# GINE layer 0: rows beside four pairs of blocks, edges beside the pair ahead, sums carried pair by pair

## The chip, the cores and the metric

The kernel runs on one core of a Trainium2 chip. The metric is the device time of one launch in microseconds (us); the figure for the kernel before is the median of three runs. The engines are named as in the profile: PE (TensorE: matmuls and transposes), DVE (VectorE), ACT (ScalarE), POOL (GpSimd, which also issues the gathers), SP (SyncE, which issues the other transfers). Each engine takes its instructions in the order in which the program has them, and waits at one whose inputs are not there.

## The reference, cut to what matters

The program has four stages on x of 10000 nodes by 512 features in float32: a relational graph network, a mixture of experts, a GINE network of four layers, and a quantized feed-forward layer. Each adds its result to x and takes the layer norm of x as its input. The change lies in the third:

```python
def _gine_layer(x, src, dst, edge_attr, eps, We, be, W1, b1, gamma, beta, W2, b2):
    e = edge_attr @ We + be
    m = jax.nn.relu(x[src] + e)
    agg = jax.ops.segment_sum(m, dst, num_segments=x.shape[0])
    h = ((1.0 + eps) * x + agg) @ W1 + b1
    mu = jnp.mean(h, axis=0)
    var = jnp.mean(jnp.square(h - mu), axis=0)
    h = (h - mu) * jax.lax.rsqrt(var + BN_EPS) * gamma + beta
    h = jax.nn.relu(h)
    return jax.nn.relu(h @ W2 + b2)
```

There are 5000 edges, sorted by target (dst). The first layer's x is the layer norm of what the mixture of experts left. The mean and variance run over all nodes, so the second product (W2) starts only when the first (W1) is done for every node.

## The kernel before, in words

**Layout.** The features lie transposed in SBUF in one tile, `big` (named feat in the profile): 128 partitions, four feature chunks, 10000 node columns. Nodes are permuted so that those with edges come first: 40 edge tiles of 128 slots feed exactly the first 5120 columns, tile t the 128 columns from 128 t. The columns are worked in ten *pairs* (of blocks of 512): pairs 0 to 8 have 1024 columns, pair 9 has 784. Pairs 0 to 4 are the ones that edges feed; the order of work is 5, 6, 7, 8, 9, 0, 1, 2, 3, 4. A copy of the rows, node by node, is kept in DRAM as `xg_d`, for the edges to gather x[src] from.

**Layer 0's rows** (loop over `order`, L1472 its transposes). A block of four tiles of 128 nodes is gathered into `x_in` (POOL, `gather`, L612), normalized (`layernorm`: statistics L168 and L169 and the scaling L183 on DVE, the square root L171 on ACT), stored to `xg_d` (SP, L137) and transposed on PE through PSUM into `big` (L1472; evictions alternate between ACT L156 and DVE L158). `x_in` has two buffers. A buffer is free again when its block is stored and transposed.

**Edges** (`gine_edge_tile`). For each tile: gather 128 rows of `xg_d` (L612), add attr x We (DVE, L1232), in layer 0 also `be` (POOL, L1234; later layers have it in the rows), relu (ACT, L1235). A 128 x 128 matrix `same`, which marks edges of one target, sums them: in layer 0 it is made from a transpose of the keys on PE (L1241) and a comparison (DVE, L1242) and stored; later layers load it. Four matmuls (L1246) give the sums in PSUM; DVE adds them into `big` with (1 + eps) x (L1250; the last column apart, L1254), and ACT keeps the last column as the tile's tail (L1258). PSUM tiles of edges, row transposes and key transposes share the name ps_x and two buffers. An edge tile's gather needs all of `xg_d`; its result is needed by the product of the pair that it feeds.

**Carry** (`gine_carry`). Sums of one target may run over tiles. A scan on DVE over all 40 tails (L1267 to L1277) carries them on and adds them to the first column of the next tile.

**Products** (`product`). Each pair's 512 x 512 product is done with seven half-size products (a scheme of Strassen's kind), 56 PE instructions of 512 columns, all on L1311; ps_b, ps_d and ps_e are its PSUM tiles. It begins with two subtractions on DVE (L1334, L1335), has two operations on POOL (L1346, L1359), evictions on ACT (L1319) and sums on DVE (L1324 or L1326); for the first product, batch-norm statistics follow (L1394). It is a Python generator of seven steps.

**What sets the order.** `products` walks the generators of an order of pairs, starts each before the last step of the one ahead, and advances `beside` between steps. In layer 0 the program text has all rows first, then pairs 5 to 9 with the 40 edge tiles beside them, the carry, and pairs 0 to 4 with nothing beside; layers 1 to 3 have the same without the rows (theirs are written by the second product of the layer ahead, `gine_second`, `row_tile` L1419 to L1422). A scheduler then orders the instructions of each engine by its own reckoning: in layer 0 it put the products of pairs 5 to 9 among the rows, all but the end of pair 9. The engines' queues that matter here: POOL has gathers, the addition of `be` and two operations of every product; SP has the stores to `xg_d`, those of `same`, and loads of weights.

Of the kernel before, what the change touches and what calls it, by code (L numbers as in the profile page):

```python
# [30 lines left out]
PAIRS = [(p * 1024, 512) for p in range(N // 1024)] + [(N // 1024 * 1024, N % 1024 // 2)]  # L31
EB = EDGE_SLOTS // 512
# [30 lines left out]
def block_cols(b):  # L63
    return min(512, N - b * 512)
# [3 lines left out]
def gnn_ffn_kernel(ctx: ExitStack, tc: tile.TileContext, I, out, dram):  # L68
# [1158 lines left out]
    def gine_edge_tile(l, t, wk, px, we, be, scaled, tails):  # L1227
# [30 lines left out]
        nc.scalar.copy(tails[:, :, t], ps_a[:, :, P - 1])  # L1258

    def gine_carry(wk, tails):  # L1260

        co, _, passes, enters = (
            by_dst["carried"][:, i, None, :].to_broadcast([P, KC, ET]) for i in range(4)
        )
        through = wk.tile([P, KC, ET], F32, name="through", bufs=1)
        sums = wk.tile([P, KC, ET], F32, name="sums", bufs=1)
        nc.vector.tensor_copy(through, passes)  # L1267
        nc.vector.tensor_tensor(tails, tails, co, OP.mult)
        nc.vector.tensor_tensor_scan(
            sums.rearrange("p k t -> p (k t)"), through.rearrange("p k t -> p (k t)"),  # L1270
            tails.rearrange("p k t -> p (k t)"), 0.0, OP.mult, OP.add,
        )
        nc.vector.tensor_tensor(
            tails[:, :, 1:], sums[:, :, : ET - 1], enters[:, :, 1:], OP.mult
        )
        firsts = big[:, :, P : EDGE_SLOTS : P]
        nc.vector.tensor_add(firsts, firsts, tails[:, :, 1:])  # L1277
# [91 lines left out]
    def products(order, make, beside):  # L1369


        gens = [make(p) for p in order]
        next(gens[0])
        next(beside, None)
        for i, g in enumerate(gens):
            for _ in range(5):
                next(g)
                next(beside, None)
            if i + 1 < len(gens):
                next(gens[i + 1])  # L1380
                next(beside, None)
            next(g, None)
            next(beside, None)
        for _ in beside:
            pass
# [21 lines left out]
    def norm_pair(p, sm):  # L1407
        s0, w = PAIRS[p]
        for j in (1, 0):
            for fo in range(KC):  # L1410
                norm_relu(s0 + j * w, s0 + (j + 1) * w, sm, fo)
                yield
# [11 lines left out]
    def gine_second(l, A, banks, tmp, px, rows, be, sm, order):  # L1424

        def beside():


            for i in range(len(order) + 1):
                normed = norm_pair(order[i + 1], sm) if i + 1 < len(order) else iter(())  # L1430
                tiles = iter(())
                if i:
                    s0, w = PAIRS[order[i - 1]]
                    tiles = iter(range(s0 // P, (s0 + 2 * w + P - 1) // P))
                for step in range(7):
                    for _ in range(2 if step < 2 else 1):
                        next(normed, None)
                    for t in tiles:
                        row_tile(t, px, rows, be)
                        break  # L1440
                    yield
                for t in tiles:
                    row_tile(t, px, rows, be)

        for _ in norm_pair(order[0], sm):
            pass
        products(
            order, lambda p: product(p, A, banks, tmp, 1.0, b2c[:, l], True, lambda half, j: None), beside()
        )

    stats = wl.tile([P, KC, NB, 6], F32, name="stats")
    sm = wl.tile([P, KC, 4], F32, name="bn_sm")
    order = list(range(EB, NB)) + list(range(EB))
    pairs = list(range(EB // 2, len(PAIRS))) + list(range(EB // 2))
    with ExitStack() as s:
# [339 lines left out]
```

## Time and profile before

| | us |
|---|---|
| median of three runs (4684.91 to 4697.69) | 4692.14 |
| the profiled execution's own time | 4696.59 |
| its span, from first to last instruction | 4694.8 |
| PE busy | 4073.4 (87%) |
| DVE busy | 2848.6 (61%) |
| ACT busy | 1625.7 (35%) |
| POOL busy | 1569.1 (33%) |
| mean granted PE clock | 0.921 of full |

How to read it. Busy time is summed per engine over the span. PE's tenths are shares of a slice (one fortieth of the span), the granted clock likewise. A matmul row counts PE instructions; a product of float32 operands takes two. In a list of waits the three numbers are the total wait in us, how often, and the longest. In a timeline a line has start, length, engine, source line, operation, what it wrote and read, how many were merged, and in brackets the idle time ahead of it with what ended that. In a list of groups a line has the count, then busy us and mean ns, then idle time ahead of the group by what ended it.

### The profile page before, as it was taken

What the parts mean: (1) busy time and instruction counts of PE and PEld (TensorE: products, weight loads), DVE (VectorE), ACT (ScalarE), POOL (GpSimd) and SP (SyncE); (2) the same over time, 40 slices, a digit from 0 to 9 for tenths busy, and PEclk for the clock granted to TensorE, in tenths of its full rate; (3) what the DMA queues carried; (4) which work ended last, traced back from release to release, by engine and by line L of the source; (5) the groups of instructions that cost most, each with busy time, mean ns of one, the idle gap of its engine ahead of it and who ended that gap; (6) DMA issues with size and microseconds to landing.
All of it is one profiled execution on the core that took longest, in us unless ns stands there. A gap on an engine that the chain in (4) does not pass through costs nothing.

```text
span 4694.8 us, 42564 instructions
## 1 busy us (share of the span) xinstructions
PE 4073.4 (87%) x13624; PEld 2069.6 (44%) x13624; DVE 2848.6 (61%) x5806; ACT 1625.7 (35%) x2895; POOL 1569.1 (33%) x1127
## 2 busy tenths in 40 slices
PE   6899478897999936967769999999999999999997
PEld 3434234443444413434454455545455454544443
DVE  7887855554544574647754457645576455755776
ACT  4344112233333310112222623345233542334775
POOL 3434334441000046864552113311143111422443
PEclk9899789898999867988859999999999999999998
DMA  8777654457555315985420113201241022311332
GB/s 281 242 263 235 226 114 87 85 105 198 179 171 178 136 47 103 160 174 184 151 83 16 54 75 123 57 16 68 77 122 42 18 79 85 112 30 45 109 109 97
DMA packets 292814, 556.19 MB, mean 118 GB/s; under 512 B 40912, under 2 KB 71665, under 8 KB 291567
## 3 DMA queue, kind: packets, MB, share of 16 engines
q1 hardware_dynamic: 219328, 364.67, 23.0%
q0 software_dynamic: 73264, 188.79, 17.5%
q8 instruction: 111, 1.82, 0.2%
q14 instruction: 111, 0.91, 0.1%
HBM read 292.40 MB, written 260.95 MB: 118 GB/s over the span
## 4 chain that ended last, share of the span: by engine, by line
PE 36%; DVE 9%; DMA 4%; issue 3%; ACT 3%; POOL 2%; DVEq 0%; POOLq 0%; ACTq 0%
PE ps_b L1311 14%; PE ps_d L1311 8%; PE ps_o L1567 5%; PE ps_e L1311 4%; DMA x<-xg_d,gpos 3%; PE ps_x L1419 2%; PE ps_x L1246 2%; DVE stats L1394 1%; ACT feat L1405 1%; DMA x_in<-x_d,node_at 1%; DVE x L1232 1%; DVE feat L1250 1%; PE ps_q L1635 1%; DVE feat L1326 1%; POOL x_in L612 1%
## 5 line engine op out<-in xcount | busy, mean ns | idle before, releaser
L1311 PE MATMUL ps_b<-feat,w 128*128 128x512 f32 (+1 forms) x1120 | 499.3, 587 | 25.5 <-ACT feat L1405 25.5
L1311 PE MATMUL ps_d<-feat,w_s 128*128 128x512 f32 (+1 forms) x1120 | 503.1, 590 | 14.4 <-DVE feat L1335 14.4
L1319 ACT ACTIVATE feat<-ps_b,cols 128x512 f32<-128x512 f32 (+1 forms) x300 | 204.4, 683 | 591.2 <-PE ps_b L1311 586.7
L1346 POOL TENSOR_TENSOR feat<-feat 128x1024 f32<-128x1024 f32 (+1 forms) x70 | 163.4, 2335 | 710.4 <-DVE feat L1345 701.8
L1359 POOL TENSOR_TENSOR feat<-feat,p 128x1024 f32<-128x1024 f32 (+1 forms) x70 | 178.1, 2544 | 474.3 <-ACT feat L1319 474.3
L635 DVE SCALAR_TENSOR_TENSOR w<-basis,att,w 128x2048 f32<-128x2048 f32 x116 | 315.0, 2724 | 14.7 <-DMA basis<-in_L_gnn_basis 14.7
L740 PE MATMUL ps_o<-root,xT 128*128 128x512 f32 (+1 forms) x632 | 321.1, 620 | 0.0
L1311 PEld LDWEIGHTS ps_b<-feat,w 128*128 128x128 f32 x1120 | 206.5, 192 | 241.3 <-issue 201.1
L1311 PEld LDWEIGHTS ps_d<-feat,w_s 128*128 128x128 f32 x1120 | 208.0, 194 | 227.9 <-issue 193.6
L701 PE MATMUL ps_o<-w,aT 128*128 x656 | 304.8, 609 | 0.0
L1421 DVE TENSOR_TENSOR x_rows<-ps_x,be 128x512 f32<-128x512 f32 (+1 forms) x237 | 160.7, 685 | 218.4 <-PE ps_x L1419 218.2
L916 PE MATMUL ps_n<-root,rT 128*128 128x512 f32 (+1 forms) x632 | 289.6, 614 | 0.0
L1311 PE MATMUL ps_e<-feat,w 128*128 128x512 f32 (+1 forms) x560 | 264.9, 613 | 12.5 <-DVE feat L1277 12.5
L612 POOL DMA_INDIRECT x<-xg_d,gpos x160 | 180.2, 1126 | 252.3 <-ACT x L1235 69.8
L1311 PE MATMUL ps_b<-t,w_s 128*128 128x512 f32 (+1 forms) x560 | 251.8, 591 | 3.5 <-ACT feat L1319 3.5
L1246 PE MATMUL ps_x<-same,x 128*128 128x128 f32 x1280 | 200.8, 309 | 61.6 <-DVE same L1242 33.8
L1311 PE MATMUL ps_b<-feat,w_s 128*128 128x512 f32 (+1 forms) x560 | 250.3, 586 | 3.1 <-DVE feat L1345 3.1
L1246 PEld LDWEIGHTS ps_x<-same,x 128*128 128x128 f32 x1280 | 186.1, 218 | 129.6 <-ACT tails L1258 63.5
L1405 ACT ACTIVATE feat<-feat,bn_sm 128x512 f32<-128x512 f32 (+2 forms) x320 | 237.1, 809 | 3.4 <-DVE bn_sm L1506 3.4
L1394 DVE BATCH_NORM_STATS2 stats<-feat 128x6 f32<-128x512 f32 (+1 forms) x320 | 202.4, 667 | 54.2 <-POOL feat L1359 42.0
L1345 DVE TENSOR_TENSOR feat<-feat,t 128x1024 f32<-128x1024 f32 (+1 forms) x70 | 84.0, 1200 | 233.0 <-PE ps_b L1311 233.0
L168 DVE BATCH_NORM_STATS2 ln_st<-x_in 128x6 f32<-128x512 f32 (+1 forms) x237 | 159.3, 682 | 53.3 <-DMA x_in<-x_d,node_at 49.3
(480 smaller groups left out, 7610.2 us busy)
## 6 DMA issues: line engine op xcount, KB each, us to landing
basis<-in_L_gnn_basis SPq DMA_DIRECT2D x60, 1024.0 KB
xg_d<-x_rows SPq DMA_DIRECT2D x234, 256.0 KB
x_in<-in_x SPq DMA_DIRECT2D x19, 1024.0 KB
a_d<-x_in SPq DMA_DIRECT2D x19, 1024.0 KB
xn_d<-xn SPq DMA_DIRECT2D x19, 1024.0 KB
r_d<-o_nodes SPq DMA_DIRECT2D x19, 1024.0 KB
r_in<-r_d SPq DMA_DIRECT2D x19, 1024.0 KB
x_in<-a_d SPq DMA_DIRECT2D x19, 1024.0 KB
```

Of the source, the lines that this page charges most:

```text
L612: return nc.gpsimd.indirect_dma_start(out=dst, out_offset=None, in_=src, in_offset=bass.IndirectOffsetOnAxis(ap=idx, axis=0))
L635: nc.vector.scalar_tensor_tensor(ws[:, r], tf, c, ws[:, r], op0=OP.mult, op1=OP.add)
L701: nc.tensor.matmul(ps_o, lhsT=aT[:, k, :], rhs=w_all[:, bass.ds(w0 + k * D, D)], start=k == 0, stop=k == KC - 1,)
L740: nc.tensor.matmul(ps_o[:n], lhsT=xT[:, k, a * P : a * P + n], rhs=root[:, k, :], start=k == 0, stop=k == KC - 1,)
L916: nc.tensor.matmul(ps_o[:n_], lhsT=rT[:, k, a * P : a * P + n_], rhs=root[:, k, :], start=k == 0, stop=k == KC - 1,)
L1246: nc.tensor.matmul(ps_a[:, k, :], lhsT=x[:, k * P : (k + 1) * P], rhs=same, start=True, stop=True)
L1311: nc.tensor.matmul(ps[fo], lhsT=A[a][:, k, fo * P : (fo + 1) * P], rhs=x[:, k, :], start=first and k == 0, stop=k == 1, skip_group_check=True,
L1319: nc.scalar.activation(dst[:, fo, :], ps[fo], func, bias=b, scale=scale)
L1359: nc.gpsimd.tensor_tensor(b22, b22, p5, OP.add)
L1394: nc.vector.bn_stats(stats[:, k, 2 * p + j, :], big[:, k, s0 + j * w : s0 + (j + 1) * w])
L1405: nc.scalar.activation(hb, hb, AF.Relu, bias=sm[:, fo, 3:4], scale=sm[:, fo, 2:3])
L1567: nc.tensor.matmul(ps_o[:n_], lhsT=big[:, kc, t * P : t * P + n_], rhs=W2[kc], start=kc == 0, stop=kc == KC - 1,)
```

## The change

In layer 0 the rows come in units of two tiles (`first_rows`) with four buffers, and the normalizing runs on ACT. Five units come first; the other 35 are given out over the 24 steps of pairs 5 to 8. The edge tiles that feed pair 0 stand beside pair 9, those of pair 1 beside pair 0, and so on to those of pair 4 beside pair 3; pair 4 has nothing beside it. In layers 1 to 3 edges stand beside pairs 5 to 9 as they did, eight tiles over six steps. The carry is done after each pair's eight tiles, and its last sum is handed to the next. `products` calls `beside(i, step)` instead of advancing a generator; `shared_out` splits a list evenly over steps. `gine_second` and `norm_pair` are rewritten to this form: the norm of the next pair and the row tiles of the last are given out over six steps instead of seven.

```diff
+PT = 8
+EDGE_PAIRS = EDGE_SLOTS // (PT * P)
...
-        nc.scalar.copy(tails[:, :, t], ps_a[:, :, P - 1])
-    def gine_carry(wk, tails):
+        nc.scalar.copy(tail, ps_a[:, :, P - 1])
+    def gine_carry(p, wk, tails):
+        ts = slice(p * PT, (p + 1) * PT)
         co, _, passes, enters = (
-            by_dst["carried"][:, i, None, :].to_broadcast([P, KC, ET]) for i in range(4)
+            by_dst["carried"][:, i, None, ts].to_broadcast([P, KC, PT]) for i in range(4)
         )
-        through = wk.tile([P, KC, ET], F32, name="through", bufs=1)
-        sums = wk.tile([P, KC, ET], F32, name="sums", bufs=1)
-        nc.vector.tensor_copy(through, passes)
-        nc.vector.tensor_tensor(tails, tails, co, OP.mult)
+        through = wk.tile([P, KC, PT + 1], F32, name="through")
+        sums = wk.tile([P, KC, PT + 1], F32, name="sums")
+        nc.vector.memset(through[:, :, 0], 0.0)
+        nc.vector.tensor_copy(through[:, :, 1:], passes)
+        mine = tails[:, p]
+        nc.vector.tensor_tensor(mine[:, :, 1:], mine[:, :, 1:], co, OP.mult)
         nc.vector.tensor_tensor_scan(
             sums.rearrange("p k t -> p (k t)"), through.rearrange("p k t -> p (k t)"),
-            tails.rearrange("p k t -> p (k t)"), 0.0, OP.mult, OP.add,
+            mine.rearrange("p k t -> p (k t)"), 0.0, OP.mult, OP.add,
         )
-        nc.vector.tensor_tensor(
-            tails[:, :, 1:], sums[:, :, : ET - 1], enters[:, :, 1:], OP.mult
-        )
-        firsts = big[:, :, P : EDGE_SLOTS : P]
-        nc.vector.tensor_add(firsts, firsts, tails[:, :, 1:])
+        if p + 1 < EDGE_PAIRS:
+            nc.vector.tensor_copy(tails[:, p + 1, :, 0], sums[:, :, PT])
+        nc.vector.tensor_tensor(mine[:, :, :PT], sums[:, :, :PT], enters, OP.mult)
+        firsts = big[:, :, p * PT * P : (p + 1) * PT * P : P]
+        nc.vector.tensor_add(firsts, firsts, mine[:, :, :PT])
...
     def products(order, make, beside):
-        gens = [make(p) for p in order]
-        next(gens[0])
-        next(beside, None)
-        for i, g in enumerate(gens):
-            for _ in range(5):
-                next(g)
-                next(beside, None)
-            if i + 1 < len(gens):
-                next(gens[i + 1])
-                next(beside, None)
-            next(g, None)
-            next(beside, None)
-        for _ in beside:
-            pass
+        g = None
+        for i, p in enumerate(order):
+            last, g = g, make(p)
+            next(g)
+            if last:
+                next(last, None)
+            for step in range(6):
+                beside(i, step)
+                if step < 5:
+                    next(g)
+        next(g, None)
+    def shared_out(work, step, steps):
+        return work[step * len(work) // steps : (step + 1) * len(work) // steps]
...
-    order = list(range(EB, NB)) + list(range(EB))
-    pairs = list(range(EB // 2, len(PAIRS))) + list(range(EB // 2))
+    pairs = list(range(EDGE_PAIRS, len(PAIRS))) + list(range(EDGE_PAIRS))
     with ExitStack() as s:
         banks = s.enter_context(tc.tile_pool(name="banks", bufs=1, space=PSUM))
         px = s.enter_context(tc.tile_pool(name="px", bufs=2, space=PSUM))
         tmp = s.enter_context(tc.tile_pool(name="p_tmp", bufs=1))
-        with ExitStack() as n:
-            ld = n.enter_context(tc.tile_pool(name="g0_ld", bufs=2))
-            small = n.enter_context(tc.tile_pool(name="g0_small", bufs=3))
-            for b in order:
-                tiles, parts = block_tiles(b), block_parts(b)
-                x = ld.tile([P, 4, D], F32, name="x_in")
-                for a, n_ in tiles:
-                    gather(x[:n_, a, :], x2_d, node_at[:n_, b * 4 + a : b * 4 + a + 1])
-                layernorm(small, x, x, tiles, parts)
-                rows_to(x, xg_d, b, store=True)
+        def first_rows(t0, ld, small):
+            tiles = [(a, min(P, N - (t0 + a) * P)) for a in range(2) if t0 + a < NT]
+            n = tiles[0][1]
+            x = ld.tile([P, 2, D], F32, name="x_in")
+            for a, n_ in tiles:
+                gather(x[:n_, a, :], x2_d, node_at[:n_, t0 + a : t0 + a + 1])
+            layernorm(small, x, x, tiles, [(n, 0, len(tiles))], on_act=True)
+            r0 = t0 * P
+            nc.sync.dma_start(
+                xg_d[r0 : r0 + n * len(tiles), :].rearrange("(a p) d -> p a d", p=n), x[:n, : len(tiles), :]
+            )
+            for a, n_ in tiles:
+                ps_t = px.tile([P, KC, P], F32, name="ps_x")
                 for k in range(KC):
-                    ps_t = px.tile([P, 512], F32, name="ps_x")
-                    for a, n_ in tiles:
-                        nc.tensor.transpose(
-                            ps_t[:, a * P : a * P + n_], x[:n_, a, k * P : (k + 1) * P], ident[:n_, :n_]
-                        )
-                    copy_out(block(k, b), ps_t[:, : block_cols(b)])
+                    nc.tensor.transpose(ps_t[:, k, :n_], x[:n_, a, k * P : (k + 1) * P], ident[:n_, :n_])
+                copy_out(big[:, :, (t0 + a) * P : (t0 + a) * P + n_], ps_t[:, :, :n_])
         for l in range(LAYERS):
             A = load_weights(l, 0)
             with ExitStack() as n:
-                wk = n.enter_context(tc.tile_pool(name=f"ge_wk_{l}", bufs=1))
-                we = row_broadcast(wk, I["L1_gnn_We"][l, 0], D, "we")
-                be = row_broadcast(wk, I["L1_gnn_be"][l], D, "be") if l == 0 else None
-                scaled = wk.tile([P, KC, ET], F32, name="scaled")
-                tails = wk.tile([P, KC, ET], F32, name="tails")
-                nc.vector.tensor_scalar(
-                    scaled, big[:, :, P - 1 : EDGE_SLOTS : P], one_eps[:, l : l + 1], None, op0=OP.mult
-                )
-                def edges():
-                    for t in range(ET):
-                        gine_edge_tile(l, t, wk, px, we, be, scaled, tails)
-                        if t % 8:
-                            yield
-                gine_first(l, A, banks, tmp, stats, pairs[: len(PAIRS) - EB // 2], edges())
-                gine_carry(wk, tails)
-            gine_first(l, A, banks, tmp, stats, pairs[len(PAIRS) - EB // 2 :], iter(()))
+                first_edges = 0
+                if l == 0:
+                    first_edges = len(PAIRS) - EDGE_PAIRS - 1
+                    n0 = n.enter_context(ExitStack())
+                    ld = n0.enter_context(tc.tile_pool(name="g0_ld", bufs=4))
+                    small = n0.enter_context(tc.tile_pool(name="g0_small", bufs=4))
+                    units = [t for p in pairs for t in range(p * PT, min((p + 1) * PT, NT), 2)]
+                    for t in units[:5]:
+                        first_rows(t, ld, small)
+                at = {}
+                def begin_edges():
+                    at["wk"] = wk = n.enter_context(tc.tile_pool(name=f"ge_wk_{l}", bufs=1))
+                    at["we"] = row_broadcast(wk, I["L1_gnn_We"][l, 0], D, "we")
+                    at["be"] = row_broadcast(wk, I["L1_gnn_be"][l], D, "be") if l == 0 else None
+                    at["tails"] = wk.tile([P, EDGE_PAIRS, KC, PT + 1], F32, name="tails")
+                    nc.vector.memset(at["tails"][:, 0, :, 0], 0.0)
+                    at["scaled"] = wk.tile([P, KC, ET], F32, name="scaled")
+                    nc.vector.tensor_scalar(
+                        at["scaled"], big[:, :, P - 1 : EDGE_SLOTS : P], one_eps[:, l : l + 1], None,
+                        op0=OP.mult,
+                    )
+                def beside(i, step):
+                    p = i - first_edges
+                    if p < 0:
+                        for t in shared_out(units[5:], i * 6 + step, first_edges * 6):
+                            first_rows(t, ld, small)
+                    elif p < EDGE_PAIRS:
+                        if p == 0 and step == 0:
+                            if l == 0:
+                                n0.close()
+                            begin_edges()
+                        for j in shared_out(range(PT), step, 6):
+                            gine_edge_tile(
+                                l, p * PT + j, at["wk"], px, at["we"], at["be"], at["scaled"],
+                                at["tails"][:, p, :, j + 1],
+                            )
+                        if step == 5:
+                            gine_carry(p, at["wk"], at["tails"])
+                gine_first(l, A, banks, tmp, stats, pairs, beside)
             for fo in range(KC):
...
```

More of the change, by code (lines that the diff above doesn't have):

```diff
@@ L1225, in block, with gine_edge_tile @@
         return big[:, k, b * 512 : b * 512 + block_cols(b)]
-    def gine_edge_tile(l, t, wk, px, we, be, scaled, tails):
+    def gine_edge_tile(l, t, wk, px, we, be, scaled, tail):
         x = wk.tile([P, D], F32, name="x", bufs=4)
@@ L1408, in norm_pair @@
         s0, w = PAIRS[p]
-        for j in (1, 0):
-            for fo in range(KC):
-                norm_relu(s0 + j * w, s0 + (j + 1) * w, sm, fo)
-                yield
+        return [(s0 + j * w, s0 + (j + 1) * w, sm, fo) for j in (1, 0) for fo in range(KC)]
     def row_tile(t, px, rows, be):
@@ L1424, in gine_second, with row_tiles @@
     def gine_second(l, A, banks, tmp, px, rows, be, sm, order):
[L1426 to L1446, printed above, removed]
+        def beside(i, step):
+            if i + 1 < len(order):
+                for c in shared_out(norm_pair(order[i + 1], sm), step, 6):
+                    norm_relu(*c)
+            if i:
+                row_tiles(order[i - 1], step, 6)
+        def row_tiles(p, step, steps):
+            s0, w = PAIRS[p]
+            for t in shared_out(range(s0 // P, (s0 + 2 * w + P - 1) // P), step, steps):
+                row_tile(t, px, rows, be)
+        for c in norm_pair(order[0], sm):
+            norm_relu(*c)
         products(
-            order, lambda p: product(p, A, banks, tmp, 1.0, b2c[:, l], True, lambda half, j: None), beside()
+            order, lambda p: product(p, A, banks, tmp, 1.0, b2c[:, l], True, lambda half, j: None), beside
         )
+        row_tiles(order[-1], 0, 1)
     stats = wl.tile([P, KC, NB, 6], F32, name="stats")
     sm = wl.tile([P, KC, 4], F32, name="bn_sm")
-    order = list(range(EB, NB)) + list(range(EB))
-    pairs = list(range(EB // 2, len(PAIRS))) + list(range(EB // 2))
+    pairs = list(range(EDGE_PAIRS, len(PAIRS))) + list(range(EDGE_PAIRS))
     with ExitStack() as s:
@@ L1489, in edges @@
-                def edges():
-                    for t in range(ET):
-                        gine_edge_tile(l, t, wk, px, we, be, scaled, tails)
-                        if t % 8:
-                            yield
-                gine_first(l, A, banks, tmp, stats, pairs[: len(PAIRS) - EB // 2], edges())
-                gine_carry(wk, tails)
-            gine_first(l, A, banks, tmp, stats, pairs[len(PAIRS) - EB // 2 :], iter(()))
+                first_edges = 0
[7 more added lines that the diff above has]
+                        first_rows(t, ld, small)
@@ new lines, in beside @@
+                def beside(i, step):
+                    p = i - first_edges
[14 more added lines that the diff above has]
+                            gine_carry(p, at["wk"], at["tails"])
@@ L1528, in gnn_ffn_kernel @@
         live, old, rows_in, stores = {}, {}, {}, []
-        first_rows = wl.tile([P, 2, D], F32, name="t3")
-        first_rows = [first_rows[:, 0, :], first_rows[:, 1, :]]
+        rows_0 = wl.tile([P, 2, D], F32, name="t3")
+        rows_0 = [rows_0[:, 0, :], rows_0[:, 1, :]]
         for name in ("s2", "s3"):
-            first_rows.append(wl.tile([P, 2, D // 2], F32, name=f"w_{name}").rearrange("p k o -> p (k o)"))
+            rows_0.append(wl.tile([P, 2, D // 2], F32, name=f"w_{name}").rearrange("p k o -> p (k o)"))
         x_1 = one.tile([P, 4, D], F32, name="x_1")
-        x0 = [first_rows, [x_1[:, a, :] for a in range(4)]]
+        x0 = [rows_0, [x_1[:, a, :] for a in range(4)]]
         def region(b):
```

## The prediction

> **What bounds the kernel now.** I began with the page. It says that TensorE (PE) is busy 87% of the span, and that in the 18th to 21st slice this is not so and the granted clock falls.
>
> ```profile
> span 4694.8 us, 42564 instructions
> PE 4073.4 (87%) x13624; PEld 2069.6 (44%) x13624; DVE 2848.6 (61%) x5806; ACT 1625.7 (35%) x2895; POOL 1569.1 (33%) x1127
> PE   6899478897999936967769999999999999999997
> PEclk9899789898999867988859999999999999999998
> ```
>
> A slice is 117 us, so these are about 2000 to 2465 us, most of GINE layer 0. The timeline gives its borders: first row gather (L612) at 2079.9, last row transpose (L1472) done at 2301.3, carry (L1277) done at 2453.3, last product done at 2573.4. The busy time by stage, with layer 1's two halves below for comparison (columns: window, length, then PE, PEld, DVE, ACT and POOL busy, clock, DMA share, GB/s):
>
> ```profile
> 2079.00:2302.00 223.00, 160.69 (x541) 85.22 (x542) 167.33 (x354) 56.37 (x99) 100.46 (x87) 0.81 0.58 193
> 2302.00:2453.00 151.00, 102.43 (x416) 78.54 (x414) 87.51 (x186) 38.12 (x92) 94.48 (x82) 0.63 0.32 91
> 2453.00:2573.00 120.00, 119.73 (x273) 53.02 (x274) 52.36 (x72) 31.40 (x47) 23.74 (x9) 0.98 0.05 14
> 2866.00:3026.00 160.00, 150.24 (x591) 87.35 (x590) 121.87 (x201) 63.09 (x129) 70.27 (x50) 0.99 0.30 86
> 3026.00:3146.00 120.00, 118.16 (x276) 52.04 (x274) 53.39 (x75) 33.45 (x50) 26.07 (x10) 1.00 0.05 16
> ```
>
> Only the third stage is PE's: five pairs in 120 us, 24.0 us each, at full clock. The first has five pairs' products beside the rows and still no engine full. The second has little but edges, at clock 0.63 (0.50 between 2360 and 2450). Layer 1 does 40 edge tiles *and* five products in 160 us, against 151 us here for the edges with only the end of one product. So layer 0's order wastes PE twice.
>
> What holds the rows? One buffer's loop, from the timeline (the first line is the block's first gather, the second its fourth, the last the next gather into the same buffer):
>
> ```profile
> 2194.18 0.96 POOL L612 DMA_INDIRECT x_in<-x_d,node_at  x1
> 2198.11 0.94 POOL L612 DMA_INDIRECT x_in<-x_d,node_at  x1 [0.30 <-issue]
> 2203.97 0.69 DVE L168 BATCH_NORM_STATS2 ln_st<-x_in 128x6 f32<-128x512 f32 x1 [0.59 <-DMA x_in<-x_d,node_at]
> 2207.69 1.91 DVE L183 TENSOR_SCALAR x_in<-x_in,ln_mv,ln_rs 128x512 f32<-128x512 f32 x4
> 2215.28 0.94 POOL L612 DMA_INDIRECT x_in<-x_d,node_at  x1 [4.77 <-DMA xg_d<-x_in]
> ```
>
> The loop is 21.1 us: 9.8 gathering (three steps of 1.25, then 5.9 to landing), 5.6 for statistics and normalizing (work 0.69 + 0.17 + 0.30 + 0.17 + 1.91 = 3.24, so 2.4 of queueing), 5.7 for the store that frees the buffer. Two buffers, 20 blocks: the last block starts after nine loops, 190 us, and needs 9.8 + 5.6 + about 3 of transposes: 208. Measured 221, 6% more. The rows are bound by the latency of two buffers.
>
> What holds the edges? PE's waits in the second stage, and the group that waits:
>
> ```profile
> PE ps_x L1246 <- DVE same L1242: 33.8, 29, 2.7
> PE ps_x L1246 <- ACT tails L1258: 7.7, 6, 1.5
> L1246 PE MATMUL ps_x<-same,x 128*128 128x128 f32 x320 | 73.3, 402 | 43.6 <-DVE same L1242 33.8 <-ACT tails L1258 7.7 <-ACT x L1235 2.1
> ```
>
> Two PSUM buffers serve alternately the key transpose and the sum, so the next tile's matmuls wait until the last sum is evicted (L1250 0.74 + L1254 0.22 + L1242 0.34 + L1258 0.17). With nothing else to issue PE idles 44 us, its clock stays halved, and a tile takes 3.4 us.
>
> **The change part by part.** In the built program's order the row transposes now lie among the products of pairs 5 to 8 and the head of pair 9; then come the edges, eight tiles a pair, beside the rest of pair 9 and pairs 0 to 3; pair 4 is alone.
>
> *Rows (first_rows).* Blocks of four tiles become 40 units of at most two, four buffers of half the size. A loop: one gather step 1.25 + 5.9; work 0.69 + 0.17 + 0.30 + 0.17 + 0.17 (the added shift, priced as the reciprocal) + 2 x 0.81 (normalizing on ACT; L179 does the same form in 0.813) = 3.1, with the same 2.4 of queueing 5.5; the store. No 512 KB store stands apart in the trace; it lies between a 256 KB gather's 4.3 and the 1 MB store's 5.7, I take 5.0. Sum 17.65. The last unit starts after nine loops (36 units, four at a time), 159 us, plus 7.15 + 5.5 + 1.5 = 173. The old stage was 6% above this reckoning; because sqrt and normalizing now stand in ACT's queue behind evictions of 0.75 us, I take 10%: 190, so rows end at 2270 instead of 2301. That is 31 us, and one product fewer rides here.
>
> Floors below that: PE 316 transposes x 0.137 (eight in 1.04 us at full clock) + 4 x 24.0 = 139; DVE 79 x 0.85 + 40 x (0.67 + 0.34) + 4 x 10.5 = 150; POOL 79 x 1.25 + 4 x 4.8 = 118. None is the bound. The 40 stores replace 21 on SP's queue, at 0.36 us of issue; nothing else is due there until the edges. On POOL the gathers stand in line with two product instructions a pair; one of these (L1359) held the gathers 10.9 us in the old order, and is in the percentage.
>
> Here a page speaks against the change. The Trainium skill, "DMA: Bandwidth & Descriptors" (Anatomy of one DMA), gives each transfer some 2.0 us fixed plus bytes over 436 GB/s, and advises 1 MiB or more. Its formula gives 4.4 us for 1 MB where the row has 5.7. If the fixed parts of some 20 more stores were paid one after another, that would add 40 us to 173 before any queueing: rows end at about 2304, no gain. I go by the loop, since one store per loop is paid and four loops run abreast.
>
> *Edges beside pairs.* Nearest row: layer 1's 160 us for 40 tiles and five products, one short. Layer 0 adds:
> - 40 key transposes on PE, 40 x 0.137 = 5.5. Their evictions (13.6 us) are on DVE, which idles 38 of 160.
> - Carries. Pair p's product now waits for carry p, just issued. The old single carry cost PE 3.2 us (layer 1's wait of ps_e on L1277), already once in the 160. Four more, less one tile of the next pair (1.1) that the order puts ahead of each product: 4 x 2.1 = 8.4. Bounds 0 and 12.8.
> - The be addition on POOL, 40 x 1.28 = 51 us, beside DVE's products. See the lines below.
>
> ```profile
> 2954.36 2.35 POOL L1359 TENSOR_TENSOR feat<-feat,p 128x1024 f32<-128x1024 f32 x1 [2.63 <-ACT feat L1319]
> 2954.75 3.04 DVE L1334 TENSOR_TENSOR t<-feat 128x1024 f32<-128x1024 f32 x1
> ```
>
> The subtraction, 1.2 us when alone, ends 1.08 us after POOL's instruction. The Trainium skill, "SBUF — State Buffer" (the part on the two sides of its ports), has the rule behind it: a GpSimd operation and a DVE operation with two SBUF inputs lock each other out for a whole instruction. In layer 1 five L1334 took 10.9 instead of 6.0, so 4.9 lost under 22.9 us of POOL arithmetic, 0.21 per us. By that row the additions cost 51 x 0.21 = 11; by the rule at its worst, every one in the path, 51; by nothing but PE, 0. I take 11.
>
> Stage: 160 + 5.5 + 8.4 + 11 = 185. Before it 8.9 us from last transpose to first edge matmul (2301.3 to 2310.2), in which the order has about 7.5 us of pair 9's product, taken off the stage. After it pair 4, 24.0. Sum 8.9 - 7.5 + 185 + 24.0 = 210, against 2573.4 - 2301.3 = 272 now: 62 us. The clock needs no term of its own: the layer-1 row ran at 0.99.
>
> *Layers 1 to 3.* Carry 0 is done four pairs before its product, so the 3.2 us wait goes, three times: 9 us. Five carries of some seven small DVE instructions replace one of five: about 5.5 us more on DVE per layer, behind 38 us of its idle time; uncovered it would be 16 in all. Eight tiles over six steps instead of seven, and the rewritten second products, issue the same instructions: nothing.
>
> Sum: 31 + 62 + 9 = 102 us. The profiled span 4694.8 becomes 4593 (its own time was 4696.6); against the median 4692.1, which lies 4.5 below that run, I forecast **4590 us**.
>
> **Rivals.**
> - *The rows stay as slow* (the page's fixed cost, or POOL's line): end at 2304. For it: gathers waited 28.7 us on stores, and DMA already runs at 0.58 of its engines. Against: that share leaves room. 4590 + 34 = 4624.
> - *POOL and DVE get in each other's way beside the products*: the additions cost 51, not 11. For it: DVE would be busy about 150 of 185. 4630.
> - *PE becomes the bound throughout*: rows need 139 + 14, end at 2233 (37 less), edges stall on neither carries nor additions (19 less). For it: layer 1's 150 of 160. Against: 21 us loops with four buffers don't feed it. 4534.
> - *Slower: the carries clog DVE's queue.* Twenty pairs (five a layer) now meet a carry in DVE's line; its first instruction waits for ACT's copy of the last tail, and evictions of products stand behind it. It turns the sign from 102/20 = 5.1 us a pair; at 8 us a pair 160 is lost: 4590 + 160 = 4750. Against: the old carry's wait for ACT was 0.3 us.
>
> **How the numbers follow.** Mine 0.54 (its own range 4566 to 4614), slow rows 0.18, POOL and DVE 0.12, PE bound 0.10, clogged 0.04, and 0.02 for mishaps that leave it within 0.3% (14 us, about what a measurement here can tell). The range 4550 to 4645 leaves out the last two and most of the PE-bound case, near 0.15. Faster 0.94, same 0.02, slower 0.04.
>
> **What would show it.** Right: row transposes end near 2270 and the last layer-0 product near 2480; clock above 0.9 throughout; PE idle in the edges 20 to 30 us; ps_e no longer waits on the carry in layers 1 to 3. Wrong: row units every 5.5 us instead of 4.4; edges at over 45 us a pair; new waits of PE on DVE in layers 1 to 3.

## The result: 0.8% faster, under half of the forecast

| | us |
|---|---|
| before, median of seven runs (4684.91 to 4712.07) | 4697.69 |
| after, median of seven runs (4653.02 to 4669.12) | 4658.12 |
| ratio after to before, 95% interval | 0.9922 [0.9903, 0.9941] |
| forecast, and its range | 4590, 4550 to 4645 |

The sign was right. The size was not: about 40 us (the interval says 28 to 46) where 102 were forecast, and the time lies outside the range.

### The profile after

The page of the changed kernel, the rows that answer to those shown of before:

```profile
span 4665.2 us, 42798 instructions
PE 4046.1 (87%) x13624; PEld 2048.0 (44%) x13624; DVE 2820.7 (60%) x5906; ACT 1679.5 (36%) x2992; POOL 1569.0 (34%) x1127
PE   6799568897999945968887999999999999999997
PEclk9899789898988866989889999999999999999998
```

The gap in layer 0 (slices 18 to 22 of the 40) has narrowed, but PE stands at 6 to 8 there, and the clock at 8 in three of the five. By stage (columns as before: window, length, busy time of PE, PEld, DVE, ACT, POOL, granted clock, DMA share, GB/s); the first window is the rows beside four pairs, the second the edges beside five pairs and the last pair, the third runs from layer 0's statistics to layer 1's (norm and second product of layer 0, edges and first product of layer 1):

```profile
2082.00:2281.00 199.00, 154.08 (x556) 81.17 (x557) 137.32 (x340) 115.14 (x199) 99.67 (x87) 0.91 0.66 215
2281.00:2534.00 253.00, 202.81 (x674) 112.05 (x673) 158.19 (x281) 65.03 (x137) 121.78 (x91) 0.87 0.22 62
2534.00:3104.00 570.00, 546.94 (x1757) 280.26 (x1756) 316.54 (x494) 216.28 (x362) 141.86 (x80) 0.99 0.20 67
```

The second row has what went wrong: 253 us where the forecast's sum was 210, at clock 0.87. No engine is full in it.

All readings below use the same four marks: first row gather, start of the last row transpose, start of layer 0's batch-norm aggregate (DVE, the bn_sm group), and that of layer 3. "Layers 1 to 3" is thus the time between the last two marks. The marks are needed because the first mark alone lay anywhere from 2069 to 2091 us in the twelve experiments' profiles, ahead of anything the change touches. In the two profiled executions:

| stage, us | before | after | moved | forecast |
|---|---|---|---|---|
| ahead of the first row gather | 2079.9 | 2082.2 | +2.3 | 0 |
| rows | 221.1 | 198.1 | -23.0 | -31 |
| rest, to layer 0's statistics (edges, last pairs) | 272.4 | 253.9 | -18.5 | -62 |
| layers 1 to 3 | 1703.9 | 1714.4 | +10.5 | -9 |
| last norm and the last stage | 417.5 | 416.6 | -0.9 | 0 |
| span | 4694.8 | 4665.2 | -29.6 | -102 |

So the forecast is short by 8 in the rows, 44 in the edges, and 20 in layers that the change was thought to leave alone but for one wait.

PE's waits in the edges' stage of the changed kernel (total us, times, longest):

```profile
PE ps_x L1248 <- DVE same L1244: 24.1, 16, 2.3
PE ps_e L1317 <- DVE feat L1283: 12.9, 5, 3.9
PE ps_x L1248 <- ACT x L1237: 9.4, 4, 4.4
PE ps_x L1248 <- ACT tails L1260: 3.4, 2, 2.0
```

They add up to 50 us in 253; the forecast had room for 20 to 30. Three suspects stand in them: the carry (L1283, its last instruction), the making of `same` between two sums (L1244), and the long chain of a tile through POOL and ACT (L1237). The chain into the product of pair 2, from the timeline, has the first and the third together:

```profile
2416.22 0.72 DVE L1234 SCALAR_TENSOR_TENSOR x<-we,srt_d,x 128x512 f32<-128x512 f32 x1
2416.24 1.82 POOL L1236 TENSOR_TENSOR x<-x,be 128x512 f32<-128x512 f32 x1 [0.75 <-DVE x L1234]
2416.86 1.23 DVE L1280 COPY tails<-sums 128x4 f32<-128x4 f32 x1
2418.01 0.18 DVE L1281 TENSOR_TENSOR tails<-sums,carried 128x32 f32<-128x32 f32 x1
2418.76 1.78 DVE L1283 TENSOR_TENSOR feat<-feat,tails 128x32 f32<-128x32 f32 x1
2419.19 1.27 POOL L1236 TENSOR_TENSOR x<-x,be 128x512 f32<-128x512 f32 x1
2420.60 2.08 PE L1317 MATMUL ps_e<-feat,w 128*128 128x512 f32 x2 [3.02 <-DVE feat L1283]
```

A copy of four columns takes 1.23 us and ends as POOL's addition ends; an addition of 32 columns, 0.19 us at its shortest (the group's minimum is 185 ns), takes 1.78 and ends as the next one does. And when PE goes on, it goes on slowly: two instructions of ps_e in 2.08 us.

### The profile page after: what moved, and what is told of

It reads as the page before. It is cut to its first block, busy times and chain, and to the rows that moved or that the text cites. A ratio compares the mean times of both kernels' runs of the same rounds, so it can differ in the third digit from the quotient of the medians.

```text
span 4665.2 us, 42798 instructions
## 1 busy us (share of the span) xinstructions
PE 4046.1 (87%) x13624; PEld 2048.0 (44%) x13624; DVE 2820.7 (60%) x5906; ACT 1679.5 (36%) x2992; POOL 1569.0 (34%) x1127
## 4 chain that ended last, share of the span: by engine, by line
PE 38%; DVE 8%; DMA 4%; ACT 3%; issue 2%; POOL 1%; POOLq 0%; DVEq 0%; ACTq 0%
PE ps_b L1317 15%; PE ps_d L1317 8%; PE ps_o L1593 5%; PE ps_e L1317 4%; PE ps_x L1424 2%; DMA x<-xg_d,gpos 2%; PE ps_x L1248 2%; ACT feat L1413 1%; DMA x_in<-x_d,node_at 1%; DVE stats L1402 1%; DVE x L1234 1%; DVE feat L1252 1%; PE ps_q L1661 1%; DVE feat L1332 1%; DVE t L1340 0%
## 5 line engine op out<-in xcount | busy, mean ns | idle before, releaser
L1317 PE MATMUL ps_e<-feat,w 128*128 128x512 f32 (+1 forms) x560 | 264.9, 614 | 12.9 <-DVE feat L1283 12.9
L1234 DVE SCALAR_TENSOR_TENSOR x<-we,srt_d,x 128x512 f32<-128x512 f32 x160 | 139.9, 889 | 156.6 <-DMA x<-xg_d,gpos 149.5
L1248 PE MATMUL ps_x<-same,x 128*128 128x128 f32 x1280 | 176.9, 287 | 58.6 <-DVE same L1244 24.1
L1248 PEld LDWEIGHTS ps_x<-same,x 128*128 128x128 f32 x1280 | 167.9, 199 | 126.9 <-issue 42.2
L1237 ACT ACTIVATE x<-x 128x512 f32<-128x512 f32 x160 | 99.3, 628 | 295.2 <-DVE x L1234 179.3
```

Source lines behind the costliest of these rows:

```text
L1234: nc.vector.scalar_tensor_tensor(x, we, by_dst["attr"][:, t : t + 1], x, op0=OP.mult, op1=OP.add)
L1248: nc.tensor.matmul(ps_a[:, k, :], lhsT=x[:, k * P : (k + 1) * P], rhs=same, start=True, stop=True)
L1317: nc.tensor.matmul(ps[fo], lhsT=A[a][:, k, fo * P : (fo + 1) * P], rhs=x[:, k, :], start=first and k == 0, stop=k == 1, skip_group_check=True,
```

## The experiments

Theory C says that the carry, now directly ahead of the product that needs it, took the gain; theory P that POOL's addition of `be` did; theory S that the two PSUM buffers, shared by key transposes and sums, did. Times are medians against runs of the kernel before on the same chip; where only one profiled run was made, the stages are read. "Rest" is the third row of the table above.

### The carry left out in layer 0

```diff
-                        if step == 5:
+                        if step == 5 and l:
                             gine_carry(p, at["wk"], at["tails"])
```

> The changed kernel with the carry of layer 0 left out (its five calls; sums that run over two tiles are then not added, layers 1 to 3 keep theirs). Theory C (the carry, now just ahead of the product that needs it, is what kept the edges' stage at 254 us instead of 210): the five waits of ps_e on the carry (12.9 us in the profile of the changed kernel) go, and so does the half clock that follows each of them (ps_e takes 6.5 us instead of 3.4, some 15 us in all): 25 to 30 us less, about 4630. Theory P (POOL's addition of be and its lock on DVE): the waits move to the next edge tile, 0 to 6 us less. Theory S (two PSUM buffers, one of them for the sums): likewise 0 to 6 us less.

Measured: 4630.33 us, ratio to before 0.9876 [0.9859, 0.9893]. The rest of layer 0 took 227.5 instead of 253.9: 26 us. PE's instructions of ps_e at the head of three pairs, first in the changed kernel, then without the carry:

```profile
2324.57 6.47 PE L1317 MATMUL ps_e<-feat,w 128*128 128x512 f32 x8 [0.55 <-DVE feat L1283]
2372.41 6.45 PE L1317 MATMUL ps_e<-feat,w 128*128 128x512 f32 x8 [2.91 <-DVE feat L1283]
2467.65 6.61 PE L1317 MATMUL ps_e<-feat,w 128*128 128x512 f32 x8 [3.94 <-DVE feat L1283]
```

```profile
2379.41 1.88 PE L1317 MATMUL ps_e<-feat,w 128*128 128x512 f32 x4
2382.13 1.88 PE L1317 MATMUL ps_e<-feat,w 128*128 128x512 f32 x4
```

Eight instructions in 2 x 1.88 = 3.8 us against 6.5, which over the five pairs is 12 us. Behind the carry PE works at half its clock, but the wait on the carry is not all that slows it. Short stretches around the second of these heads show it (columns as before; PE busy is the first figure behind the length, the clock the third from the end):

```profile
2364.40:2367.75 3.35, 1.52 (x11) 1.33 (x12) 3.32 (x9) 1.83 (x5) 2.48 (x3) 1.00 0.37 102
2367.80:2371.20 3.40, 1.69 (x9) 1.29 (x7) 3.08 (x7) 0.63 (x1) 2.42 (x3) 0.50 0.38 97
2374.65:2377.95 3.30, 3.30 (x5) 1.27 (x4) 2.84 (x5) 0.47 (x1) 2.20 (x2) 0.50 0.07 20
2378.10:2381.40 3.30, 3.30 (x9) 1.46 (x8) 0.00 (x0) 1.24 (x3) 0.57 (x1) 1.00 0.00 0
```

The clock was at half from about 2367.8, before the wait on the carry began at 2369.5: two waits of 1.6 us of the last two tiles had come first. It came back when the head was nearly done.

Over the whole stage, in the changed kernel and without the carry:

```profile
2280.30:2534.20 253.90, 203.71 (x679) 112.67 (x678) 159.09 (x283) 65.86 (x139) 121.78 (x91) 0.87 0.22 62
2265.70:2493.20 227.50, 187.21 (x679) 100.66 (x678) 150.64 (x248) 65.27 (x139) 123.52 (x91) 0.96 0.24 70
```

The same 679 PE instructions take 16 us less of PE's time at the higher clock, and PE's idle time falls by 10, since some other waits grow. Theory C holds for this part. This run takes away more than the carry's work, though: a head need no longer wait for the last tile, whose sums now stand between the two lines of four.

### The carry one step ahead

```diff
-                        for j in shared_out(range(PT), step, 6):
+                        for j in shared_out(range(PT), step, 6 if l else 4):
...
-                        if step == 5:
+                        if step == (5 if l else 3):
                             gine_carry(p, at["wk"], at["tails"])
```

> The changed kernel, but in layer 0 a pair's eight edge tiles are given out over the first four of the six steps and the carry follows the fourth, so that two steps of the product ahead (7 us of PE) lie between a carry and the product that needs it. Nothing is left out. Theory C: the wait and the half clock go, 20 to 30 us less than the changed kernel, about 4633. Theories P and S: the tiles stand closer together, so waits between tiles grow; no gain, or up to 10 us more.

Measured: 4633.56 us, ratio 0.9883 [0.9866, 0.9901]; rest 234.2, so 20 us less, with nothing left out. PE's waits on the carry fall from 12.9 to 6.9, and the stage's clock is 0.93 instead of 0.87. At four of the five heads it holds at full; two of these, and the sum of the waits:

```profile
2349.50 3.70 PE L1317 MATMUL ps_e<-feat,w 128*128 128x512 f32 x8 [1.55 <-DVE feat L1283]
2391.31 3.70 PE L1317 MATMUL ps_e<-feat,w 128*128 128x512 f32 x8 [1.55 <-DVE feat L1283]
PE ps_e L1317 <- DVE feat L1283: 6.9, 5, 1.6
```

Most of the cost was the place of the carry, not the work in it.

### be left out, then be on DVE

```diff
-                    at["be"] = row_broadcast(wk, I["L1_gnn_be"][l], D, "be") if l == 0 else None
+                    at["be"] = None
```

> The changed kernel without the addition of be on POOL in layer 0's edges (left out, so the sums lack it). Theory P: 40 additions of 1.28 us, their lock on DVE and their place in the chain of every tile go: 25 to 40 us less than the changed kernel. Theory C: only the waits on ACT's relu (9.4 us) shrink and the carry runs unlocked (its last instruction 0.2 us instead of up to 1.8): 8 to 14 us less. Theory S: under 8 us.

Measured: 4631.45 us, ratio 0.9883 [0.986, 0.9906]; rest 229.3, 25 us less. The sum for theory C was too low (8 to 14), that for P just met. Leaving an operation out doesn't tell whether its engine or its work costs, so it was moved:

```diff
-            nc.gpsimd.tensor_tensor(x, x, be, OP.add)
+            nc.vector.tensor_tensor(x, x, be, OP.add)
```

> The changed kernel with layer 0's addition of be on DVE instead of POOL. Leaving the addition out took 25 us off the 254. If the lock between POOL and DVE and the longer chain of a tile are its price: about 20 of the 25 us come back here, 234. If DVE's own load is the limit (it then has 40 additions of 0.7 us more, 187 us busy in all): 245 to 265.

One profiled run, 4637.55 us: rest 229.3, the same as with no addition at all, though DVE is now busy 172.60 of 229.00 us in it. PE's waits there:

```profile
PE ps_x L1248 <- ACT x L1237: 19.7, 6, 3.7
PE ps_x L1248 <- DVE same L1244: 18.2, 14, 1.6
PE ps_e L1317 <- DVE feat L1283: 2.6, 1, 2.6
```

The waits on the carry fell from 12.9 to 2.6. POOL's additions no longer hold up DVE's small instructions; the carry's last one, over the five carries of layer 0 (shortest, median and longest in ns), first in the changed kernel, then here:

```profile
L1283 DVE TENSOR_TENSOR feat<-feat,tails x5: 211/1455/1784, 2324.3 to 2511.1; 128x32 f32<-128x32 f32 x5
L1283 DVE TENSOR_TENSOR feat<-feat,tails x5: 207/208/215, 2310.8 to 2480.5; 128x32 f32<-128x32 f32 x5
```

The tiles' own chain still makes PE wait, and such a wait slows the next head just as one on the carry did:

```profile
2353.35 0.80 PE L1248 MATMUL ps_x<-same,x 128*128 128x128 f32 x2 [3.70 <-ACT x L1237]
2353.94 5.90 PE L1317 MATMUL ps_e<-feat,w 128*128 128x512 f32 x8
```

DVE's load was not the limit; the addition's place on POOL was. How much of the 25 us is the lock, and how much a tile's longer way through POOL's queue, no run separates.

### Both left out

This kernel has both edits above that leave something out, the carry's and be's.

> The changed kernel with layer 0's carry and its addition of be both left out. Each alone took 25 us off the 254 (to 227.5 and 229). If they are separate costs: 254 - 26 - 25 = 203. If they are one cost seen twice (the additions lock DVE while it does the carry): 220 to 227.

One profiled run, 4615.07 us: rest 203.2. The sum of separate costs was 203. The same 679 PE instructions now take 180 us, at clock 0.98:

```profile
2278.80:2482.00 203.20, 179.94 (x679) 99.47 (x678) 145.63 (x249) 66.91 (x139) 68.19 (x51) 0.98 0.27 77
```

What remains is mostly the wait for `same`:

```profile
PE ps_x L1248 <- DVE same L1244: 16.4, 15, 2.7
PE ps_d L1317 <- DVE feat L1341: 3.9, 4, 1.8
PE ps_x L1248 <- ACT x L1237: 3.0, 1, 3.0
```

### same made beside the rows

The three instructions of `same` move into a helper called beside pairs 5 to 8, with a tile of its own, and the edge tile loads the result as later layers do:

```diff
-        if l:
-            nc.sync.dma_start(same, same_d[:, t, :])
-        else:
-            ps_k = px.tile([P, P], F32, name="ps_x")
...
+        nc.sync.dma_start(same, same_d[:, t, :])
...
+                        for t in shared_out(range(ET), i * 6 + step, first_edges * 6):
+                            make_same(t)
```

> The changed kernel, but layer 0's matrices same (key transpose on PE, comparison on DVE, store) are made beside the rows, and its edge tiles load them as those of the later layers do. Nothing is left out. Read by stage: the changed kernel took 198 us for the rows and 254 us from the last row transpose to the statistics. Theory S (the two PSUM buffers alternate between key transpose and sum, so a sum waits for the comparison, 24 us of waits of ps_x on same): those waits go and 254 becomes 225 to 232; the rows take 0 to 8 us more. Theory C: 254 stays above 248, since the carry's waits and the half clock after them stay.

One profiled run, 4649.88 us: rest 224.7, 29 us less, but rows 211.9, 14 more. Theory S holds for the edges: no sum waits for `same` any more. But PE's idle time fell by only 10 of the 24 us of those waits (waits for evictions of products, 17 us, stood in their place); the other 19 us are PE's own time, the 40 key transposes (12.4 us in the changed kernel) and the clock. It doesn't come free beside the rows, where 0 to 8 us more were expected: there the key transposes share the two PSUM buffers with the row transposes, which waited 15.1 us on `same`.

### Layers 1 to 3: the tiles at seven places

`products` gets a further call, between the start of a product and the last step of the one ahead; in layers 1 to 3 tile 0 goes there, tiles 1 and 2 to step 0, and one tile to each of the other five steps, as the kernel before had them.

```diff
             next(g)
+            if ahead:
+                ahead(i)
             if last:
                 next(last, None)
...
-                        for j in shared_out(range(PT), step, 6):
+                        for j in shared_out(range(PT), step, 6) if l == 0 else range(step + 2 if step else 1, step + 3):
```

> The changed kernel, but in layers 1 to 3 the eight edge tiles of a pair are given out at seven places, as in the kernel before (one of them between the start of a product and the last step of the one ahead), instead of over six steps with two pairs of neighbours. Layers 1 to 3 took 1714 us from statistics to statistics in the changed kernel, 1704 before. If the spacing of the tiles is the cause: 12 to 20 us less, since the wait for the single carry is gone too. If the five carries in DVE's line are the cause: 0 to 3 us less.

Measured: 4628.05 us, ratio 0.9867 [0.9851, 0.9884]; layers 1 to 3 took 1693.1 instead of 1714.4, 21 us less, and 11 less than the kernel before. PE's waits in the edges of layer 1, first in the changed kernel, then with seven places:

```profile
PE ps_b L1317 <- ACT feat L1325: 7.8, 4, 2.7
PE ps_x L1248 <- ACT x L1237: 3.2, 3, 1.4
PE ps_x L1248 <- ACT tails L1260: 2.0, 1, 2.0
```

```profile
PE ps_x L1248 <- ACT x L1237: 5.5, 4, 1.8
PE ps_x L1248 <- ACT tails L1260: 2.0, 1, 2.0
```

In the six-step order PE waits, once in each of four pairs, at one of the seven half-size products, until ACT has evicted the one ahead of it from the PSUM bank that both use (ps_b). With seven places that wait is gone; by which step the other spacing avoids it was not followed. The five carries, which both kernels have, cost nothing that shows here.

### The rows: three buffers, and the normalizing on DVE

```diff
-                    ld = n0.enter_context(tc.tile_pool(name="g0_ld", bufs=4))
+                    ld = n0.enter_context(tc.tile_pool(name="g0_ld", bufs=3))
```

> The changed kernel with three buffers for layer 0's row units instead of four. If the rows are bound by the loop of a buffer (17.65 us by the forecast's reckoning, thirteen loops for 40 units instead of nine): 198 becomes 250 to 265. If PE and the queues bind them (PE is busy 83% of the middle of that stage at clock 0.95): 198 to 215.

One run, 4686.11 us, rows 218.4. Neither theory is met squarely: below the 250 of the loop, just above the 215 of the queues. With thirteen loops, and 14 us for the last unit as in the forecast, a loop is (218.4 - 14) / 13 = 15.7 us; with four buffers (198.1 - 14) / 9 = 20.4. A loop that grows with more buffers is not what binds alone: with four buffers PE was busy 140.65 of the stage's middle 170 us, at clock 0.95, and part of a loop is waiting for it.

```diff
-            layernorm(small, x, x, tiles, [(n, 0, len(tiles))], on_act=True)
+            layernorm(small, x, x, tiles, [(n, 0, len(tiles))])
```

> The changed kernel with the normalizing of layer 0's rows on DVE again, as before the change. If ACT's slower instruction (0.80 us for 0.55) and its queue hold the rows: 198 becomes 185 to 192. If DVE's load matters more (137 of 199 us busy, 44 us more with it) or its lock with the gathers: 205 to 220.

One run, 4652.68 us, rows 195.8. Seven other profiles with the changed kernel's own rows show 191.3 to 196.7, itself 198.1. No difference can be read, and neither expectation is met.

### Together

All that leaves nothing out: early carry, be on DVE, `same` beside the rows, seven places.

> All of it that leaves nothing out: layer 0's tiles over four steps with the carry a step ahead, same made beside the rows, be added on DVE, and in layers 1 to 3 the tiles at seven places as before. If the causes are separate: layer 0 from the last row transpose to the statistics 254 - 20 - 20 - 10 = about 205, layers 1 to 3 1693 instead of 1714, so some 65 us under the changed kernel: about 4590. If they are one cost: 225 and 4610.

Measured: 4600.07 us, ratio 0.9792 [0.9771, 0.9812]; rows 210.6, rest 196.1, layers 1 to 3 1694.3. The edges came out 9 us better than the sum (205), the rows worse, and the time 10 us above the forecast of separate causes. To see whether `same` is worth its place, the same without it:

> The changed kernel with the tiles over four steps and the carry a step ahead in layer 0, be added on DVE, and the seven places in layers 1 to 3; same is made in the edge tiles again, as in the changed kernel. The version with same beside the rows took 210.6 us for the rows and 196 for the rest of layer 0. If the three causes are separate: rows 195, the rest 254 - 20 - 25 = 209, layers 1 to 3 1693: the same sum, about 4600. If same was the one that mattered: the rest 225, about 4613.

Measured: 4607.11 us, ratio 0.9809 [0.9791, 0.9827]; rows 196.7, rest 223.2. So the gains of an early carry (20) and of be on DVE (25) do not add: 31 together. PE's waits show what takes over once both are in:

```profile
PE ps_x L1248 <- DVE same L1244: 18.6, 13, 3.1
PE ps_e L1317 <- DVE feat L1283: 10.1, 5, 3.3
```

Tiles packed into four steps stand back to back, and back to back each waits for `same`; the carry behind them is late again. Only with `same` gone does the rest fall under 200. The last run therefore kept it out of the edges and took it out of the rows' way, into `big`'s still empty columns while the first gathers fly:

```diff
+                    for q in range(EDGE_PAIRS):
+                        same = big[:, q % KC, 3072 + q // KC * 1024 : 4096 + q // KC * 1024].rearrange(
+                            "p (t c) -> p t c", c=P
+                        )
+                        for j in range(PT):
+                            t = q * PT + j
+                            ps_k = px.tile([P, P], F32, name="ps_x")
+                            nc.tensor.transpose(ps_k, by_dst["kr"][:, t : t + 1].to_broadcast([P, P]), ident)
+                            nc.vector.tensor_scalar(
+                                same[:, j, :], ps_k, by_dst["key"][:, t : t + 1], None, op0=OP.is_equal
+                            )
+                        nc.sync.dma_start(same_d[:, q * PT : (q + 1) * PT, :], same)
```

> As the version with everything in it (early carry, be on DVE, seven places in layers 1 to 3), but the 40 matrices same are made ahead of the rows, while the first gathers are under way and PE has nothing to do for about 28 us, into columns of big that are not filled yet, and go to DRAM in five stores. If same beside the rows was what lengthened them (212 and 211 instead of 194 to 198): rows 195 to 205 by the same reading, the rest 196 as before, 4588 to 4594. If the making only moves (some 24 us of DVE turns in line ahead of the first rows): 4600 again.

Measured: 4588.00 us, ratio 0.9779 [0.9749, 0.9809], the fastest of all. By stage, rows and rest:

```profile
2080.00:2280.00 200.00, 167.15 (x592) 88.08 (x593) 147.59 (x379) 115.48 (x199) 95.90 (x87) 0.89 0.69 226
2280.00:2479.50 199.50, 178.61 (x638) 100.09 (x637) 158.47 (x283) 66.72 (x139) 68.52 (x51) 0.96 0.28 79
```

Layer 0 is 399 us in all, 53 less than in the changed kernel, with the edges at clock 0.96 instead of 0.87; layers 1 to 3 take 1692.0, 22 less.

## Why the prediction was right or wrong

**What bounds it: right.** Layer 0 did waste PE twice, and laying rows and edges beside products is worth about what was forecast, once the edges don't stall: the last version lands at 4588. That it is the forecast's own number is in part luck: it gains 21 us in the rows and 73 in the rest, for 31 and 62, and has `same` out of the edges, which the forecast left in. The changed kernel as it was got 40% of the gain.

**Rows, -31 forecast, -23 measured: near in size, by luck.** The forecast put the bound at a buffer's loop of 17.65 us. With three buffers a loop takes 15.7 by its own reckoning; nine of these and 14 us for the last unit would be 155, so with four buffers the loop is not the bound, and that 190 lies next to the 191 to 198 measured is luck. The feared fixed cost of twice as many stores did not appear: the rows end at 2280, where it put them at 2304, and DMA moved 215 GB/s against 193. (The section that the forecast names gives its formula for transfers that GpSimd issues; these stores are issued by SyncE.) Normalizing on ACT, priced with 4% more queueing, cost nothing that can be read. What exactly holds the rows at 190 to 200 us stays open.

**The edges, 185 us for the stage and 210 to the statistics: wrong, in four terms of one sum.** By its own lines the 210 hold 180 us of PE's work (150.2 of layer 1, 5.5 of key transposes, 24.0 of pair 4) and 30 of idle time. Measured were 203.7 and 50.2: 24 us of slower work and 20 of waiting. Its own sign of being wrong, edges at over 45 us a pair, came: from head to head 47.8, 48.2, 47.1 and 43.7.
- *"The clock needs no term of its own"* is the step that failed most plainly. The forecast took 0.99 from layer 1, where PE was busy 150 of 160 us. Here it was busy 203.7 of 253.9, the clock was 0.87, and the same 679 instructions took 24 us longer than the 179.9 they need at 0.98 with carry and be left out. The Trainium skill, "TensorE: Matmul & The Clock Gate" (Part 1, the clock gate), says that the clock is halved after an idle window of about 3.4 us and comes back after one as long of steady work. The traces agree that the clock is halved and comes back, but not that one idle wait of that length is needed. With be left out, ps_e took 6.76 us behind a wait of 1.29; with an early carry and be on DVE together it ran at full clock behind a wait of 2.15, where PE had worked without a break for some 15 us before:

```profile
2412.33 3.70 PE L1317 MATMUL ps_e<-feat,w 128*128 128x512 f32 x8 [2.15 <-DVE feat L1283]
```

Several short waits close together went ahead of the drops looked at; in the stretch of 3.35 us ahead of the one shown above, PE was busy for 1.52. How little work it takes, no run isolates.
- *The carry, 8.4 us.* Measured 26 when it is left out, 16 of them PE's own slower time; 20 when it comes a step earlier. The forecast took the old carry's 3.2 us less one tile; it did not see that POOL's additions would now lie in the carry's way.
- *be, 11 us.* Measured 25 (left out or moved to DVE alike). The lock was named and shown, but its rate came from a subtraction of 1.2 us; carry instructions of 0.15 to 0.21 us took 1.2 to 1.8 when an addition was under way. The forecast's bound was 51; 25 lies midway.
- *The key transposes, 5.5 us of PE.* Taking `same` out of the edges brought 29, not all of it from its waits. The forecast had shown the waits of 33.8 us on `same` itself, then priced only the transposes and took the stage from layer 1, where both PSUM buffers serve the sums. The wait that it described for the old stage went over into the new one, 24.1 us of it.

The 26, 25 and 29 are what each change gives alone. They overlap, the clock above all, and don't add up to the 44 us missed: an early carry and be on DVE gave 31 together, and with `same` moved as well 58, where the three alone sum to 74.

**Layers 1 to 3, -9 forecast, +10.5 measured: wrong at "the same instructions: nothing".** The carry's wait of 3.2 us a layer did go: with the old spacing the layers take 10.8 less than before. But the tiles' new spacing, six steps for seven places, cost 7 us a layer in waits for a PSUM bank.

**Rivals.** None came as written. *POOL and DVE in each other's way* was closest: its mechanism was at work in the carries and in the tiles; with the 25 us measured in place of 11 it gives 4604, still under the 4658. *Slow rows* did not happen; *PE bound throughout* needs the stalls gone, and even the last version is not there. *Clogged carries* was the wrong place: in layers 1 to 3, where most of it was set, five carries cost nothing that shows; in layer 0 they cost PE by being late.

## What to carry to other kernels

When a stage is moved beside another, take its stalls along in the sum: price the wait that was shown, not only the busy time of the instruction named in it. A small chain of DVE instructions in front of a matmul costs its length, what another engine's lock adds to its links, and, where other short waits stand close by, PE's slow clock as well, so put it a step earlier than needed. A stage's clock belongs in its sum: a clock read where PE hardly waits does not hold where it waits often. How often work is handed out between the steps of a product is part of the kernel: one place less per product cost 7 us a layer here.

## What the hardware showed unexpectedly

A DVE copy of 128 x 4 elements took 1.23 us, and an addition of 128 x 32 took 1.78 instead of 0.19, each ending as a POOL addition of 128 x 512 ended. Eight matmul instructions took 6.45 us instead of 3.7 behind a wait of 2.9, and 5.90 behind none, with a wait of 3.7 one step earlier; behind a wait of 2.15, with steady work ahead of it, they took 3.70.
